# Writing out the first two and the last two steps of a software-pipelined graph network kernel

## The chip, the cores and the metric

The kernel runs on one core of one Trainium2 chip. The metric is the device time of one execution in microseconds (us), as the median of several executions. TensorE does the matrix products, VectorE the elementwise work and the transposes of 32x32 blocks, ScalarE the activations and copies with a scale, GpSimd some additions, and SyncE issues most DMAs. Each engine runs its own queue in order, and engines wait for each other by semaphores.

In the profile the engines are PE (TensorE), PEld (its weight loads), DVE (VectorE), ACT (ScalarE), POOL (GpSimd) and SP (SyncE); a trailing q, as in SPq, marks an engine's sequencer issuing DMAs. A label such as `L342` is a line of that kernel's own source. So the same statement has different line numbers in different kernels.

## The reference, cut to what matters

For each of 128 graphs with 128 nodes and 512 features (`x`), and a weighted 128x128 adjacency matrix (`adj`):

```python
h = relu(layernorm(x))
# layer 0: two hypergraph convolutions, hidden width 1024
#   conv(z, W, b) = Dinv * H @ (Binv * H.T @ (z @ W.T)) + b,   H = (adj != 0)
h = relu(conv(h, W1, b1))
h = layernorm(h, gamma, beta)
x = x + (conv(h, W2, b2) + x_in)         # x_in: what layer 0 was given
# layer 1: mean over neighbours
h = relu(layernorm(x))
out = x + relu(concat([h, adj @ h / deg]) @ W.T)
```

All is float32. The weights W1, W2 and W of layer 1 are `w1`, `w2`, `w3` below, 2 MB each.

## The kernel before

Two graphs make a pair, and there are 64 pairs (`NP`). Each weight product of a pair is done by seven block products instead of eight: `seven()` runs them in the order p1, p2, p6, p5, p7, p4, p3, with three PSUM banks A, B, C. It adds sums of weight blocks (t1 to t4), made once by `weight_sums`. Four of the products (p1, p6, p7, p4) go into A one after the other, and what stands there must be copied out before the next may write:

```python
    for name, dst, lhs, rhs, first in (
        ("p1", A, "a11", "b11", True),  ("p2", Bb, "a12", "b21", True),
        ("p6", A, "s2", "t2", False),   ("p5", Cc, "s1", "t1", True),
        ("p7", A, "s3", "t3", False),   ("fill", None, None, None, None),
        ("p4", A, "a22", "t4", False),  ("p3", Cc, "s4", "b22", False),
    ):          # ... after each: background work of other pairs, then the hook that evicts the bank
```

The smaller products between them appear in the tables by the names of their PSUM tiles: `ps_s` makes the matrix `s` of a pair from its adjacency, `pz` multiplies it with the normalised features, `py` multiplies it with the result of conv2, and `pc` multiplies beta with w2 (the beta products, once). conv1(1) is conv1 of pair 1, and so on.

So the third product (p6) waits for ScalarE's copy of p1, and ScalarE comes to that copy only when it is through with all that stands ahead in its queue.

A step `t` has three such stages: the weights of conv1 of pair t, those of conv2 of pair t-1 and those of layer 1 of pair t-2. Into each, work of other pairs is threaded as "background". Between conv1 and conv2 of a pair, the result is normalised, transposed in blocks, written to DRAM and read back as `nt`. The transpose buffer `bt` has one copy, so the second transpose of a pair waits until the first one's write has landed:

```python
    def inner_transpose(p, g):
        t = pool.tile([P, Q, B, KH], FP, tag="bt", name="bt", bufs=1)
        nc.vector.transpose(...)                          # 32x32 blocks
        d = dram.tile([P, DH], FP, tag="nd", name="n_scratch")
        nc.sync.dma_start(out=d, in_=t...)                # 512 KB
        nt = pool.tile([P, P, KH], FP, tag="nt", name="nt")
        for jj in range(Q):
            nc.sync.dma_start(out=nt[...], in_=d...)      # 4 x 128 KB
```

The schedule was a loop with a short preamble:

```python
    with tc.manual_schedule():
        load_w1(); load_w2()           # both issued by ScalarE
        load(0); load(1); load_small() # issued by SyncE: adj, adj in blocks (adjb), x
        # ... preparation of pairs 0 and 1 ...
        step(0)
        step(1, [prepare_w2, lambda: weight_sums(w3, nc.gpsimd)])
        for t in range(2, NP + 3):
            step(t)
```

Of the kernel before, what the change touches and what calls it, by code (L numbers as in the profile page):

```python
# [7 lines left out]
FP = mybir.dt.float32  # L8
# [12 lines left out]
def gnn_kernel(  # L21
# [23 lines left out]
    nc = tc.nc  # L45
# [34 lines left out]
    def load(p):  # L80
        pair = slice(2 * p, 2 * p + 2)
        ADJ[p] = pool.tile([P, 2, P], FP, tag="adj", name="adj_t")
        ADJB[p] = pool.tile([P, 2, P], FP, tag="adjb", name="adjb")
        X[p] = pool.tile([P, 2, D], FP, tag="x", name="x_t", bufs=4)
        nc.sync.dma_start(out=ADJ[p], in_=adj[pair].rearrange("g c e -> c g e"))
        load_blocks(ADJB[p], adj[pair])
        nc.sync.dma_start(out=X[p], in_=x[pair].rearrange("g c d -> c g d"))

# [12 lines left out]
    w1, w2, w3 = operands("w1", 2, 512), operands("w2", 4, 256), operands("w3", 2, 512)  # L101
    BLOCKS = (("b11", 0, 0), ("t3", 0, 1), ("b22", 1, 1), ("b21", 1, 0))

    def load_w1():
        for m, rows, cols in BLOCKS:
# [3 lines left out]
                .rearrange("(k p) h -> p k h", p=P))  # L109

    def load_small():
        nc.sync.dma_start(out=b1_bc, in_=b1.partition_broadcast(P))
        for jj in range(Q):
            for i, v in enumerate((gamma, beta)):
                src = v.rearrange("(l a) (j h) -> j a h l", a=B, j=Q)[jj]
                for h in range(2):
                    nc.sync.dma_start(out=gb[B * jj : B * (jj + 1), i, 4 * h : 4 * h + 4],
                                      in_=src[:, h, :])
        nc.sync.dma_start(out=b2_bc, in_=b2.partition_broadcast(P))

    def load_w2():
        for jj in range(Q):
            src = w2t.rearrange("(j k a) o -> j a k o", j=Q, a=B)[jj]
            for m, rows, cols in BLOCKS:
                nc.scalar.dma_start(
                    out=w2[m][B * jj : B * (jj + 1)],
                    in_=src[:, 4 * rows : 4 * rows + 4, 256 * cols : 256 * cols + 256])
# [17 lines left out]

    def prepare_w2():
        pc = small_bank("pc")
        for k in range(KH):
            betas = pool.tile([P, P], FP, tag="betas", name="betas")
            nc.vector.tensor_copy(betas, gb[:, 1, k : k + 1].to_broadcast([P, P]))  # L150
            for cols, ms in enumerate((("b11", "b21"), ("t3", "b22"))):
# [3 lines left out]
        nc.vector.tensor_copy(c0, pc)  # L155
        for m, rows in (("t3", 0), ("b11", 0), ("b22", 1), ("b21", 1)):
            for k in range(4):
                nc.scalar.activation(w2[m][:, k, :], w2[m][:, k, :], AF.Copy,
                                     scale=gb[:, 0, 4 * rows + k : 4 * rows + k + 1])
        weight_sums(w2, nc.vector)  # L160

# [95 lines left out]
    def prep_norm(p, g):  # L257
        rs = RS[1, p]
        if g == 0:
            H0[p] = pool.tile([P, 2, D], FP, tag="h0", name="h0", bufs=1)  # L260
        nc.scalar.activation(H0[p][:, g, :], X[p][:, g, :], AF.Relu,
                             bias=rs[:, 1, g : g + 1], scale=rs[:, 0, g : g + 1])
# [56 lines left out]
    def conv1_weights(p, bg, fill):  # L319
        dn = DN[p]  # L320
        ra, rb = (pool.tile([P, DH], FP, tag="r", name="r") for _ in range(2))
        R[p] = [ra, rb]
# [114 lines left out]
    def layer1_transpose(p, g):  # L437
# [6 lines left out]
        if p not in H3T:  # L444
            H3T[p] = pool.tile([P, 2, P, KD], FP, tag="h3t", name="h3t")
        for jj in range(Q):
# [69 lines left out]

    def step(t, mid=()):
        run(conv1_weights, t, [
# [9 lines left out]
        ], at(t - 3, aggregate) + at(t + 1, node_matrix))  # L528
        for f in mid:
            f()  # L530
        run(conv2_weights, t - 1, [
            at(t, inner_relu, 1) + at(t + 2, prep_adj),
            at(t, stats, 2, 1),
# [5 lines left out]
            at(t, inner_norm, 0) + at(t, inner_transpose, 1),  # L539
        ], at(t + 1, conv1_nodes))  # L540
        run(layer1_weights, t - 2, [
            at(t + 2, prep_incidence, 1) + at(t + 1, residual, 1),
# [8 lines left out]

    with tc.manual_schedule():
        load_w1()
        load_w2()
        load(0)
        load(1)
        load_small()
        prep_incidence(0, 0)
        prep_incidence(0, 1)
        stats(0, 1, 0)  # L560
        stats(0, 1, 1)
        scales(0, 1)
        prep_norm(0, 0)
        prep_norm(0, 1)
        node_matrix(0)
        weight_sums(w1, nc.vector)
        conv1_nodes(0)
        conv1_left(0)
        load_w3()
        residual(0, 1)  # L570
        residual(0, 0)
        prep_incidence(1, 0)
        prep_incidence(1, 1)
        stats(1, 1, 0)
        stats(1, 1, 1)
        scales(1, 1)
        prep_adj(0)
        prep_ant(0)
        prep_adj(1)
        step(0)  # L580
        step(1, [prepare_w2, lambda: weight_sums(w3, nc.gpsimd)])
        for t in range(2, NP + 3):
            step(t)

# [33 lines left out]
```

## Time and profile before

| | before |
|---|---|
| median time (range, runs) | 2809.39 us (2808.28 to 2809.93, 4) |
| span of the profiled execution | 2805.3 us, mean TensorE clock 0.989 |
| TensorE busy | 2706.3 us (96%) |
| first matmul / first product of conv2 of pair 1 | 11.85 / 158.90 us (159.06 in the view of the chain, which the prediction uses) |
| last pair's conv2 starts / its last stage starts | 2737.66 / 2783.01 us |

The page's overview shows where the idle time of TensorE lies. Each digit is the busy share (PE) or the granted clock (PEclk), in tenths, of one fortieth of the span, here some 70 us:

```profile
PE   3689999999999999999999999999999999999996
PEclk8899999999999999999999999999999999999998
```

Only the first three slices and the last one are not full. The prediction cuts these open.

### The profile page before, as it was taken

The numbers are of one execution on the slowest core, as the hardware profiler recorded it, in microseconds if no ns is written. First come the engines' busy times: TensorE is split into PE (matmuls) and PEld (weight loads), VectorE is DVE, ScalarE is ACT, GpSimd is POOL, SyncE is SP. The second block draws the span as 40 slices with busy tenths as digits, with TensorE's granted clock in tenths as the row PEclk, the third lists the DMA queues.
The fourth block names the chain that finished last, engine by engine and source line by source line (L and its number), as shares of the span: only waits on it lengthen the run. The fifth ranks groups of instructions, "written<-read, shape, count | busy, mean of one in ns | idle before, by whom it ended". The sixth has DMA issues, their size and how long they took to land.

```text
span 2805.3 us, 29702 instructions
## 1 busy us (share of the span) xinstructions
PE 2706.3 (96%) x8992; PEld 1702.1 (61%) x8992; DVE 2100.7 (75%) x3920; ACT 1124.3 (40%) x1745; POOL 1024.4 (37%) x922
## 2 busy tenths in 40 slices
PE   3689999999999999999999999999999999999996
PEld 1456665665665665665665665666666666666563
DVE  3677777877777777777777777777777777777753
ACT  1343443443343443343444444444444444444331
POOL 3433433433333333333333343343343343343331
PEclk8899999999999999999999999999999999999998
DMA  6233333333333333334333334333333333333321
GB/s 146 68 105 114 114 111 117 114 107 120 116 102 122 116 101 123 117 104 126 113 102 124 113 103 124 111 106 123 111 115 114 113 113 113 114 113 111 105 98 53
DMA packets 400127, 311.10 MB, mean 111 GB/s; under 512 B 166752, under 2 KB 332640, under 8 KB 399968
## 3 DMA queue, kind: packets, MB, share of 16 engines
q1 hardware_dynamic: 395808, 302.92, 35.1%
q10 hardware_dynamic: 3392, 4.20, 0.6%
q0 software_dynamic: 768, 2.10, 0.3%
q8 instruction: 72, 1.18, 0.2%
q14 instruction: 87, 0.71, 0.1%
HBM read 166.47 MB, written 142.61 MB: 110 GB/s over the span
## 4 chain that ended last, share of the span: by engine, by line
PE 94%; DMA 2%; DVE 2%; SPq 1%; issue 0%; ACT 0%; DVEq 0%; ACTq 0%
PE pA L187 46%; PE pC L187 23%; PE pB L187 11%; PE pz L301 4%; PE py L421 4%; PE pB L491 2%; PE pA L490 2%; PE ps_s L278 1%; DMA n_scratch<-bt 1%; DMA adjb<-in_adj_dram 0%; DVE bt L358 0%; DMA nt<-n_scratch 0%; DMA h_scratch<-hbt 0%; DVE st L167 0%; PE pc L152 0%
## 5 line engine op out<-in xcount | busy, mean ns | idle before, releaser
L390 POOL TENSOR_TENSOR ns<-na,ns 128x512 f32<-128x512 f32 x64 | 81.9, 1279 | 767.2 <-DVE ns L386 706.3
L187 PE MATMUL pA<-w1t,zs 128*128 128x512 f32 x512 | 246.5, 604 | 25.6 <-ACT r L339 25.5
L358 DVE STREAM_TRANSPOSE bt<-r 128x1024 f32<-128x1024 f32 x128 | 261.0, 2039 | 5.6 <-DMA n_scratch<-bt 5.6
L187 PE MATMUL pA<-w2t,ns 128*128 128x256 f32 x1024 | 242.1, 379 | 0.7 <-ACT g L409 0.7
L187 PE MATMUL pA<-w3t,hs 128*128 128x512 f32 x512 | 240.6, 592 | 0.0
L335 POOL TENSOR_TENSOR r<-r,b_bc 128x512 f32<-128x512 f32 x128 | 163.6, 1278 | 166.2 <-DVE r L333 163.5
L187 PEld LDWEIGHTS pA<-w2t,ns 128*128 128x128 f32 x1024 | 194.4, 190 | 27.8 <-ACT g L409 1.5
L348 ACT ACTIVATE r<-r 128x1024 f32<-128x1024 f32 x128 | 135.3, 1057 | 170.2 <-DVE r L343 135.3
L187 PEld LDWEIGHTS pA<-w1t,zs 128*128 128x128 f32 x512 | 98.2, 193 | 151.9 <-issue 125.7
L378 ACT ACTIVATE na<-nt 128x512 f32<-128x512 f32 x64 | 72.6, 1135 | 285.9 <-DMA nt<-n_scratch 285.9
L266 POOL TENSOR_TENSOR x_t<-x_t,b_bc 128x512 f32<-128x512 f32 x128 | 166.7, 1303 | 10.0
L187 PEld LDWEIGHTS pA<-w3t,hs 128*128 128x128 f32 x512 | 97.3, 190 | 114.9 <-issue 107.1
L167 DVE BATCH_NORM_STATS2 st<-r 128x6 f32<-128x512 f32 x256 | 162.9, 675 | 0.2 <-ACT r L348 0.2
L265 POOL TENSOR_TENSOR x_t<-x_t,h 128x512 f32<-128x512 f32 x128 | 162.8, 1272 | 0.0
L301 PE MATMUL pz<-s,h 128*128 128x128 f32 x1024 | 129.9, 281 | 32.9 <-ACT s L282 20.2
L330 POOL TENSOR_TENSOR r<-r,b_bc 128x512 f32<-128x512 f32 x64 | 81.3, 1270 | 213.0 <-DVE r L329 198.7
L352 ACT ACTIVATE r<-r,rs 128x1024 f32<-128x1024 f32 x128 | 158.2, 1236 | 0.3 <-DVE rs L175 0.3
L457 POOL TENSOR_TENSOR hs<-hs,h3t 128x256 f32<-128x256 f32 x64 | 74.2, 1160 | 225.4 <-DVE hs L455 189.1
L301 PEld LDWEIGHTS pz<-s,h 128*128 128x128 f32 x1024 | 128.4, 197 | 38.2 <-ACT s L282 20.5
L440 DVE STREAM_TRANSPOSE hbt<-h 128x512 f32<-128x512 f32 x128 | 141.5, 1118 | 7.1 <-ACT h L434 2.3
L172 ACT ACTIVATE sd<-mv,eps 128x2 f32<-128x2 f32 x192 | 56.1, 292 | 203.2 <-DVE mv L168 203.2
L187 PE MATMUL pA<-w3b,h3t 128*128 128x512 f32 x256 | 122.9, 603 | 12.9 <-DMA h3t<-h_scratch 12.9
(128 smaller groups left out, 5941.8 us busy)
## 6 DMA issues: line engine op xcount, KB each, us to landing
n_scratch<-bt SPq DMA_DIRECT2D x128, 512.0 KB, 2.7
nt<-n_scratch SPq DMA_DIRECT2D x512, 128.0 KB, 2.8
x_t<-in_x_dram SPq DMA_DIRECT2D x64, 512.0 KB, 3.7
h_scratch<-hbt SPq DMA_DIRECT2D x128, 256.0 KB, 2.1
h3t<-h_scratch SPq DMA_DIRECT2D x512, 64.0 KB, 1.9
out_dram<-x SPq DMA_DIRECT2D x64, 512.0 KB, 2.9
adj_t<-in_adj_dram SPq DMA_DIRECT2D x64, 128.0 KB, 3.1
adjb<-in_adj_dram SPq DMA_DIRECT2D x256, 32.0 KB, 2.4
```

The costliest lines, as they stand in the source:

```text
L167: nc.vector.bn_stats(st[:, i, :], src[:, i * 512 : (i + 1) * 512])
L187: nc.tensor.matmul(dst, left[lhs](k), w[rhs][:, k, :], start=(first and k == 0), stop=(k == kk - 1), skip_group_check=True)
L265: nc.gpsimd.tensor_tensor(X[p][:, g, :], X[p][:, g, :], H0[p][:, g, :], ADD)
L266: nc.gpsimd.tensor_tensor(X[p][:, g, :], X[p][:, g, :], b2_bc, ADD)
L301: nc.tensor.matmul(z[:, k * P : (k + 1) * P], h[:, g, k * P : (k + 1) * P], S[p][:, g, :], start=True, stop=True)
L335: nc.gpsimd.tensor_tensor(ra[:, h], ra[:, h], b1_bc[:, h], ADD)
L348: nc.scalar.activation(R[p][g], R[p][g], AF.Relu)
L352: nc.scalar.activation(R[p][g], R[p][g], AF.Identity, bias=rs[:, 1, g : g + 1], scale=rs[:, 0, g : g + 1])
L358: nc.vector.transpose(t.rearrange("p j b k -> p j k b"), R[p][g].rearrange("p (j k b) -> p j k b", j=Q, k=KH))
L390: nc.gpsimd.tensor_tensor(l[m], l["a12"], l["s2"], SUB)
L421: nc.tensor.matmul(py, s[:, i, :], g[:, i, :], start=True, stop=True)
L440: nc.vector.transpose(t.rearrange("p j b k -> p j k b"), H3[p][:, g, :].rearrange("p (j k b) -> p j k b", j=Q, k=KD))
```

## The change

The intent: the loop body suits the middle, but the pipe fills and drains in it badly. The changed kernel writes the first two steps (`head`) and the last two (`tail`) out by hand and keeps the loop for the rest. Five things move: ScalarE no longer issues the loads of w2; x is loaded ahead of adj; conv1 of pair 1 comes directly behind conv1 of pair 0; the scaling of w2 by gamma is threaded through conv1 of pair 1; and at the end the work between the last pair's conv2 and its last stage runs beside the products of the pair before it. Two buffers are traded: `r` gets three, `h3t` one. Two moves more are in the diff: the beta products go from behind conv1(1) to ahead of it, and the loads of w3 now stand behind `second(1, 2)`.

```diff
     def load(p):
-        nc.sync.dma_start(out=ADJ[p], in_=adj[pair]...)
-        load_blocks(ADJB[p], adj[pair])
-        nc.sync.dma_start(out=X[p], in_=x[pair]...)
+        nc.sync.dma_start(out=X[p], in_=x[pair]...)
+        load_blocks(ADJB[p], adj[pair])
+        nc.sync.dma_start(out=ADJ[p], in_=adj[pair]...)
 ...
     def load_small():        # 8 small loads of gamma and beta instead of 16, b2 last
 ...
     def load_w2():
-                nc.scalar.dma_start(
+                nc.sync.dma_start(
 ...
-        ra, rb = (pool.tile([P, DH], FP, tag="r", name="r") for _ in range(2))
+        ra, rb = (pool.tile([P, DH], FP, tag="r", name="r", bufs=3) for _ in range(2))
 ...
-            H3T[p] = pool.tile([P, 2, P, KD], FP, tag="h3t", name="h3t")
+            H3T[p] = pool.tile([P, 2, P, KD], FP, tag="h3t", name="h3t", bufs=1)
 ...
+    def head():
+        load_w1(); load(0); <b1>; load(1); load_w2(); load_small()
+        <statistics, incidence and norm of pair 0>
+        node_matrix(0); conv1_nodes(0); weight_sums(w1, nc.vector); conv1_left(0)
+        conv1_weights(0, <background: residual of pair 0, preparation of pair 1>)
+        conv1_nodes(1); conv1_left(1)
+        <two relus, statistics, scale of pair 0>
+        beta_products()
+        <norms and transposes of pair 0>
+        conv1_weights(1, <background: the four scalings of w2, preparation of pair 2, w2 sums>)
+        conv2_left(0, ...)
+        second(1, 2)
+        load_w3(); weight_sums(w3, nc.gpsimd); prep_ant(2); prep_adj(3)
+        third(1)
+    def tail(t):
+        conv2_nodes(t - 1)
+        run(layer1_weights, t - 2, <background: conv2_out, statistics, norm, transposes of pair t-1>)
+        aggregate(t - 2); layer1_left(t - 1); finish(t - 2)
+        layer1_weights(t - 1, ...); aggregate(t - 1); finish(t - 1)
 ...
-        step(0)
-        step(1, [prepare_w2, lambda: weight_sums(w3, nc.gpsimd)])
-        for t in range(2, NP + 3):
-            step(t)
+        head()
+        for t in range(2, NP):
+            first(t); second(t); third(t)
+        first(NP); second(NP); tail(NP)
```

More of the change, by code (lines that the diff above doesn't have):

```diff
@@ L81, in load @@
         pair = slice(2 * p, 2 * p + 2)
+        X[p] = pool.tile([P, 2, D], FP, tag="x", name="x_t", bufs=4)
+        ADJB[p] = pool.tile([P, 2, P], FP, tag="adjb", name="adjb")
         ADJ[p] = pool.tile([P, 2, P], FP, tag="adj", name="adj_t")
-        ADJB[p] = pool.tile([P, 2, P], FP, tag="adjb", name="adjb")
-        X[p] = pool.tile([P, 2, D], FP, tag="x", name="x_t", bufs=4)
+        nc.sync.dma_start(out=X[p], in_=x[pair].rearrange("g c d -> c g d"))
+        load_blocks(ADJB[p], adj[pair])
         nc.sync.dma_start(out=ADJ[p], in_=adj[pair].rearrange("g c e -> c g e"))
-        load_blocks(ADJB[p], adj[pair])
-        nc.sync.dma_start(out=X[p], in_=x[pair].rearrange("g c d -> c g d"))
     b1_bc = const.tile([P, DH], FP, name="b1_bc")
@@ L101, in gnn_kernel @@
     w1, w2, w3 = operands("w1", 2, 512), operands("w2", 4, 256), operands("w3", 2, 512)
-    BLOCKS = (("b11", 0, 0), ("t3", 0, 1), ("b22", 1, 1), ("b21", 1, 0))
+    BLOCKS = (("b11", 0, 0), ("b21", 1, 0), ("t3", 0, 1), ("b22", 1, 1))
     def load_w1():
@@ L111, in load_small, with vector_of @@
     def load_small():
-        nc.sync.dma_start(out=b1_bc, in_=b1.partition_broadcast(P))
         for jj in range(Q):
-            for i, v in enumerate((gamma, beta)):
-                src = v.rearrange("(l a) (j h) -> j a h l", a=B, j=Q)[jj]
-                for h in range(2):
-                    nc.sync.dma_start(out=gb[B * jj : B * (jj + 1), i, 4 * h : 4 * h + 4],
-                                      in_=src[:, h, :])
+            for i, v in enumerate((beta, gamma)):
+                nc.sync.dma_start(
+                    out=gb[B * jj : B * (jj + 1), i].rearrange("a (l h) -> a l h", h=2),
+                    in_=v.rearrange("(l a) (j h) -> j a l h", a=B, j=Q)[jj])
         nc.sync.dma_start(out=b2_bc, in_=b2.partition_broadcast(P))
+    def vector_of(i, k):
+        c = 2 * (k % 4) + k // 4
+        return gb[:, i, c : c + 1]
     def load_w2():
@@ L124, in load_w2 @@
             for m, rows, cols in BLOCKS:
-                nc.scalar.dma_start(
+                nc.sync.dma_start(
                     out=w2[m][B * jj : B * (jj + 1)],
@@ L144, in gnn_kernel, with beta_products @@
     c0 = const.tile([P, D], FP, name="c0")
-    def prepare_w2():
-        pc = small_bank("pc")
+    def beta_products():
+        pc = bank("pc")
         for k in range(KH):
             betas = pool.tile([P, P], FP, tag="betas", name="betas")
-            nc.vector.tensor_copy(betas, gb[:, 1, k : k + 1].to_broadcast([P, P]))
+            nc.vector.tensor_copy(betas, vector_of(0, k).to_broadcast([P, P]))
             for cols, ms in enumerate((("b11", "b21"), ("t3", "b22"))):
@@ L155, in prepare_w2, with scale_w2 @@
         nc.vector.tensor_copy(c0, pc)
-        for m, rows in (("t3", 0), ("b11", 0), ("b22", 1), ("b21", 1)):
-            for k in range(4):
-                nc.scalar.activation(w2[m][:, k, :], w2[m][:, k, :], AF.Copy,
-                                     scale=gb[:, 0, 4 * rows + k : 4 * rows + k + 1])
-        weight_sums(w2, nc.vector)
+    def scale_w2(m, rows):
+        for k in range(4):
+            nc.scalar.activation(w2[m][:, k, :], w2[m][:, k, :], AF.Copy,
+                                 scale=vector_of(1, 4 * rows + k))
     def ln_stats(src, mv, tag):
@@ L258, in prep_norm @@
         rs = RS[1, p]
-        if g == 0:
+        if p not in H0:
             H0[p] = pool.tile([P, 2, D], FP, tag="h0", name="h0", bufs=1)
@@ L515, in run, with first @@
                 f()
-    def step(t, mid=()):
+    def first(t):
         run(conv1_weights, t, [
@@ L528, in step, with second @@
         ], at(t - 3, aggregate) + at(t + 1, node_matrix))
-        for f in mid:
-            f()
+    def second(t, adj_of=None):
         run(conv2_weights, t - 1, [
-            at(t, inner_relu, 1) + at(t + 2, prep_adj),
+            at(t, inner_relu, 1) + at(t + 2 if adj_of is None else adj_of, prep_adj),
             at(t, stats, 2, 1),
@@ L540, in step, with third @@
         ], at(t + 1, conv1_nodes))
+    def third(t):
         run(layer1_weights, t - 2, [
@@ L550, in step @@
         ], at(t - 1, conv2_nodes))
-    with tc.manual_schedule():
+    def head():
         load_w1()
+        load(0)
+        nc.sync.dma_start(out=b1_bc, in_=b1.partition_broadcast(P))
+        load(1)
         load_w2()
-        load(0)
-        load(1)
         load_small()
+        for g in range(2):
+            stats(0, 1, g)
+        scales(0, 1)
         prep_incidence(0, 0)
         prep_incidence(0, 1)
-        stats(0, 1, 0)
-        stats(0, 1, 1)
-        scales(0, 1)
-        prep_norm(0, 0)
-        prep_norm(0, 1)
+        for g in range(2):
+            prep_norm(0, g)
@@ L565, in gnn_kernel @@
         node_matrix(0)
+        conv1_nodes(0)
         weight_sums(w1, nc.vector)
-        conv1_nodes(0)
         conv1_left(0)
-        load_w3()
-        residual(0, 1)
-        residual(0, 0)
-        prep_incidence(1, 0)
-        prep_incidence(1, 1)
-        stats(1, 1, 0)
-        stats(1, 1, 1)
-        scales(1, 1)
-        prep_adj(0)
-        prep_ant(0)
-        prep_adj(1)
-        step(0)
-        step(1, [prepare_w2, lambda: weight_sums(w3, nc.gpsimd)])
-        for t in range(2, NP + 3):
-            step(t)
+        conv1_weights(0, [
+            at(0, residual, 1) + at(0, residual, 0) + at(1, prep_incidence, 0),
+            at(1, prep_incidence, 1),
+            at(1, stats, 1, 0),
+            at(1, stats, 1, 1) + at(1, scales, 1),
+            at(0, prep_adj) + at(2, load),
+            at(1, prep_norm, 1),
+            at(1, prep_norm, 0),
+            [],
+        ], at(1, node_matrix))
@@ new lines, in head @@
+        conv1_nodes(1)
+        conv1_left(1)
+        inner_relu(0, 1)
+        stats(0, 2, 1)
+        inner_relu(0, 0)
+        stats(0, 2, 0)
+        scales(0, 2)
+        beta_products()
+        for g in (1, 0):
+            inner_norm(0, g)
+            inner_transpose(0, g)
+        conv1_weights(1, [
+            [lambda: scale_w2("b11", 0)] + at(0, prep_ant),
+            at(2, prep_incidence, 0) + at(2, prep_incidence, 1) + at(1, prep_adj) + at(3, load),
+            [lambda: scale_w2("t3", 0)] + at(2, stats, 1, 0),
+            at(2, stats, 1, 1) + at(2, scales, 1),
+            [lambda: scale_w2("b22", 1)] + at(1, residual, 1) + at(1, residual, 0),
+            [lambda: scale_w2("b21", 1)],
+            [lambda: weight_sums(w2, nc.vector)],
+            at(1, prep_ant),
+        ], at(2, node_matrix))
@@ new lines, in head @@
+        conv2_left(0, "a11", "a12", "s1", "s3", "s2", "s4", "a22")
+        second(1, 2)
+        load_w3()
+        weight_sums(w3, nc.gpsimd)
+        prep_ant(2)
+        prep_adj(3)
+        third(1)
+    def tail(t):
+        p = t - 1
+        conv2_nodes(p)
+        run(layer1_weights, t - 2, [
+            [],
+            at(p, conv2_out, 1) + at(p, conv2_out, 0) + at(p, stats, 3, 1) + at(p, stats, 3, 0),
+            at(p, scales, 3),
+            at(p, layer1_norm, 1) + at(p, layer1_norm, 0),
+            at(p, layer1_transpose, 1) + at(p, layer1_transpose, 0),
+            [],
+            [],
+            [],
+        ], [])
+        aggregate(t - 2)
+        layer1_left(p)
+        finish(t - 2)
+        layer1_weights(p, [[]] * 8, [])
+        aggregate(p)
+        finish(p)
@@ L587 @@
+    with tc.manual_schedule():
+        head()
+        for t in range(2, NP):
+            first(t)
+            second(t)
+            third(t)
+        first(NP)
+        second(NP)
+        tail(NP)
 _OUT = ((128, 128, 512), "float32")
```

## The prediction

> **What bounds the kernel now.** I first cut the span into three stretches, in the view of busy time by stretch (per engine: busy us and instructions; then TensorE clock, DMA share, GB/s).
>
> ```profile
> 0.00:160.00 160.00, 84.01 (x246) 50.52 (x247) 82.18 (x159) 42.70 (x72) 60.23 (x57) 0.85 0.42 109
> 160.00:2710.00 2550.00, 2549.86 (x8536) 1608.12 (x8535) 1982.01 (x3700) 1063.71 (x1645) 951.66 (x854) 1.00 0.36 113
> 2710.00:2806.00 96.00, 72.39 (x213) 43.48 (x212) 36.52 (x63) 17.89 (x28) 12.54 (x12) 0.92 0.20 68
> ```
>
> The middle is solid TensorE work at full clock (2549.86 of 2550 us). It can't get faster by reordering. What there is to win is 160 - 84.0 = 76.0 us of idle TensorE in the head, 96 - 72.4 = 23.6 in the tail (5.3 of them after its last matmul, 0.7 past the end), and the half-clock loss. For the last, the head's products at full clock, by durations from the middle of the chain: 3 x 0.45 (ps_s), 3 x 1.78 (pz), 21 x 1.72 (conv1), 7.16 (pc), 7 x 1.73 (conv2), 1.72 (py) = 63.8, against 84.0 spent. So 20 us go to the clock.
>
> Then what TensorE waited for in the head (total, times, longest) and in the tail:
>
> ```profile
> PE pA L187 <- ACT r L339: 25.5, 3, 13.2
> PE pz L301 <- ACT s L282: 20.2, 1, 20.2
> PE pz L301 <- ACT h L261: 12.7, 3, 6.1
> PE ps_s L278 <- DVE sb L255: 11.8, 1, 11.8
> ```
> ```profile
> PE pA L187 <- DMA h3t<-h_scratch: 12.9, 1, 12.9
> ```
>
> The 20.2 comes from ScalarE, which issues the w2 loads before its first activation (timeline):
>
> ```profile
> 29.41 1.28 ACT L172 ACT_TABLE_LOAD   x1 [29.41 <-DMA b_bc<-in_b_dram]
> 31.43 1.52 ACT L261 ACTIVATE h<-x_t,rs 128x512 f32<-128x512 f32 x2 [0.43 <-DVE rs L175]
> ```
>
> The other waits are order: the copy L339 stands in ScalarE's queue behind a square root or a copy of `nt` that is itself waiting. The chain of waits shows the `nt` detour, from the second transpose to the copy:
>
> ```profile
> 77.24 2.05 DVE bt L358
> 79.31 3.36 DMA n_scratch<-bt
> 83.99 2.95 DMA nt<-n_scratch
> 87.99 0.68 ACT r L339
> ```
>
> **What the Trainium skill says.** "TensorE: Matmul & The Clock Gate", Part 1: the clock falls to half after about one idle window of 3.4 us and comes back after about as long a busy one. The trace agrees: after the 12.9 us wait the first four matmuls of the last pair took 3.66 us, against 1.72 for four in the chain. "DMA: Bandwidth & Descriptors", Anatomy of one DMA: a fixed cost of about 2 us, mostly the receipt; the trace has 2.0 to 2.2 for `h_scratch`, 2.6 to 3.4 for `n_scratch`. Same page, Issuing engines are not separate DMA queues: moving a load to another queue only saves issue time. The trace agrees with the second half: the gain is ScalarE's freedom, not bandwidth (mean DMA share 0.98 from 10 to 20 us). Same page, Queues, rings and completion order: each DMA engine alternates between rings packet by packet; the 128-byte packets of `adjb` next to the 2 KB packets of w1 fit that: issued from 1.2 us, the last landed only at 9.2.
>
> **The change, part by part.** I list when stages begin, by durations of before; (n) is the pair.
>
> Start: x goes first, and ScalarE is free after w1 (about 5.5 us). x lands near 6, so statistics (1.7), square root and norm are done by 10.5, before the incidence. `adjb` now queues behind x on its ring, beside w1: I take 10.0 (estimate: 2.6 MB at the 344 GB/s seen from 4 to 8 us). Plus 2.3 on VectorE (9.50 to 11.80 before): ps_s(0) at 12.3, and 1.2 + 0.5 later pz(0) at 14.0. Before 33.3: 19.3 saved.
>
> conv1(0): zs2 ended 7.4 after pz began, so the third product starts at 22 instead of 45.6, as no square root of pair 1 is ahead of the copy now. Five products, ps_s and a copy: ends 31.8.
>
> pz(1) needs h0(1). h0 has one buffer, read by pair 0's residual on GpSimd, whose second instruction needs b2. b2 is now the last small load, behind 2 MB of w2 on one queue whose issues wait for the landing of the eighth before. I put it at 31 (29.4 before: w2 is paced at 206 GB/s from about 17 us, then eight small loads). Then 2 x 1.27 + 1.5 (two norms): pz(1) at 35.1, before 66.5.
>
> pz(1) at half clock 4.1; za copies, two relus (2 x 1.06), statistics (2 x 1.4), scale: betas at 45.1. TensorE cools again, so pc takes 7.2 + 2: conv1(1) starts at 54.4. The transposes now stand behind c0: 55.3, then 2.05 + 2.7 + 2.05 and 7.65 from the end of the second to `nt` (79.29 to 86.94 before): 69.7.
>
> conv1(1): five products, 62.9. ps_s(2) and the square root of pair 2 stand behind the second transpose (62.05) on VectorE: 0.45 + 2.3 + 1.5 + 0.75 + 1.7, then on ScalarE 0.3, four scalings of w2 (4 x 0.51) and the copy 0.7: the next product waits till 71.7, runs cold (3.65), and the stage ends at 77.1. conv2(0) starts then; before 109.0.
>
> conv2(0): ns2 stands behind the w2 sums (one beside GpSimd takes 3.2, not 1.2): third product at 83.5, last ends 93.9, py waits for GpSimd's sum: conv1(2) starts at 97.5, before 135.3.
>
> conv1(2) keeps the `nt` detour: second transpose about 98.4 to 100.4, but adj(3)'s scratch write and four reads now sit ahead on the sync queue (3.4 more): `nt` at 110.9, third product 112.6, before 146.95. From there as before (12.1): conv2(1) at 124.7 instead of 159.06. **Head: 34.4 us.** From there the order is the old one, and TensorE stays full.
>
> Tail: py goes before layer1 of the last but one pair (waits 1.2 net for GpSimd), and conv2_out, statistics, norm and transposes of the last pair run beside its products. First transpose ends near 2765.0 instead of 2773.3. The load of `h3t` now waits for its single buffer, read until the sixth product (2768.5): then 1.75 + 2.2 + 0.1 + 1.7 + 2.0: the last pair's first product at 2776.2 instead of 2783.0. From there 22.3 us, as before. **Tail: 6.8 us**, with some chance of another 1.9 if the 4.3 us gap leaves the clock up; I take 7.
>
> Sum: 34.4 + 7 = 41.4; 2808.9 - 41.4 = 2767.5, said 2767.
>
> **Rivals.** (a) b2 lands by 27: pz(1) starts at 31.8, with no cold start; 5 to 6 us more, 2762. For: 29.4 before with twice as many small loads. Against: it was not behind w2 in one queue. (b) b2 lands at 36 to 40: every stage after it moves along, 2772 to 2776. For: eight-deep gating, each w2 load 5.5 us to landing. (c) The single `h3t` buffer stalls the middle: 61 steps at even 1 us would make it slower, 2828. Against: the load was issued at 2704.3 while the last reader was done by about 2694; 10 us of slack. (d) The chained queue waits in conv1(1) and conv2(0) do not bind, or bind less: TensorE has 60 us of work there, so with 30 us of idle the middle would begin at 95 and the time be near 2740, over 2% faster. Against: each engine runs its queue in order, and the second transpose can't start before the first one's DMA has landed. (e) w3's sixteen issues (8.6) and sums (10.6) sit on GpSimd ahead of pair 2's bias sums: I get 125.4 for the first, just in time; if late by 5, 2772.
>
> **Range and chances.** The middle is measured, to a few us. The head is a chain of some fifteen links, each good to about 1 us, with b2 good to 4 and the clock windows to 2 per cold start; the tail is good to 2. I take 2754 to 2780. Over 2% faster needs 56 us (below 2752.7), possible only with (a) and much of (d): 0.07. Slower by 2% needs (c) at its worst: 0.01.
>
> **What would show it.** Right: first matmul at 12 us, pz(0) near 14, the last long wait of the head over near 113 and TensorE full from there, h3t wait of the last pair near 4 us, the middle still full. pz(1) waiting for ScalarE h, and that for GpSimd's residual, at about 35. Wrong: a TensorE idle share inside the middle, ps_s(0) later than 14, or no wait at pc.

## The result, and the profile after

| | before | after |
|---|---|---|
| median (range, runs) | 2809.39 us (2808.28 to 2809.93, 4) | 2776.55 us (2774.55 to 2778.63, 4) |
| span of the profiled execution | 2805.3 us | 2772.7 us |
| mean TensorE clock | 0.989 | 0.992 |

The outputs are right. The ratio is 0.9884, with a 95% interval of 0.9867 to 0.9901: 1.2% faster, which counts as the same at the 2% mark. Ratios here are the mean time of one kernel's fast runs over the mean of the other's fast runs of the same rounds, so they are not quite the ratio of the medians quoted. The medians of the kernel before varied from 2807.7 to 2809.8 between the calls.

The gain can be split at one event which both traces have, the first product of the last pair's conv2: it starts at 2737.66 before and at 2711.91 after, so 25.75 us came from the head and the middle. From there to the end it is 67.62 before and 60.79 after, so 6.83 us came from the tail. Together these are the 32.6 us between the spans. The view of busy time by stretch says that none of it came from the middle (columns: stretch, its length, then busy us and instructions of PE, PEld, DVE, ACT and POOL, the clock, the DMA share and GB/s):

```profile
0.00:130.00 130.00, 74.77 (x232) 46.67 (x232) 76.81 (x151) 40.60 (x69) 58.94 (x54) 0.84 0.52 128
130.00:2680.00 2550.00, 2549.77 (x8537) 1608.54 (x8538) 1982.82 (x3703) 1067.20 (x1648) 950.62 (x855) 1.00 0.36 113
2680.00:2773.00 93.00, 77.33 (x225) 45.59 (x223) 40.39 (x68) 19.09 (x30) 15.52 (x14) 0.97 0.22 76
```

The middle is as full as before (2549.77 of 2550 us); its first stage, conv2(1), begins 25.1 us earlier (133.77 for 158.90). But 55 us are still idle in the first 130. The waits of TensorE in the first 165 us, and then the one that counts in the tail (total, times, longest), answer to the two lists in the prediction:

```profile
PE pA L190 <- ACT r L342: 18.5, 1, 18.5
PE ps_s L281 <- DVE sb L258: 15.1, 2, 13.6
PE pc L155 <- DVE betas L153: 6.6, 1, 6.6
PE pA L190 <- ACT r L331: 5.9, 3, 5.2
PE pz L304 <- ACT h L264: 4.3, 1, 4.3
PE pA L190 <- DVE ns L389: 3.1, 1, 3.1
```
```profile
PE pA L190 <- DMA h3t<-h_scratch: 4.3, 1, 4.3
```

The wait of 20.2 us for ScalarE's copy of `s` is gone. The reason is in ScalarE's timeline, where the table load now stands at 7.37 us instead of 29.41, right behind the four loads of w1:

```profile
7.37 1.28 ACT L175 ACT_TABLE_LOAD   x1 [7.37 <-DMA w1b<-in_w1t_dram]
9.39 1.52 ACT L264 ACTIVATE h<-x_t,rs 128x512 f32<-128x512 f32 x2 [0.43 <-DVE rs L178]
```

But one wait is larger than expected: 18.5 us for the copy L342, ahead of the third product of conv1 of pair 2, where the times of the prediction leave 11.7. The chain of waits (start, length, what) shows what that copy waited for:

```profile
97.81 2.62 DMA n_scratch<-bt
102.33 5.85 DMA an_scratch<-adj_t
...
110.08 4.91 DMA n_scratch<-bt
116.31 4.35 DMA nt<-n_scratch
120.76 1.14 ACT na L381
121.91 0.58 ACT r L342
122.53 3.42 PE pA L190 x4
```

Read it from below: the product waits for a copy, the copy stands behind another copy of `nt`, that waits for the load of `nt`, that for the second scratch write, and that stood on the queue behind the reads of pair 3's adjacency. The write `n_scratch`, which took 2.62 us at 97.81, took 4.91 at 110.08. In between lies something new: GpSimd issued the sixteen loads of w3 from 99.31 to 109.3 us. From 103 to 109 us the mean DMA share was 1.08, against 0.52 over the first 130 us. The change itself put them there: in the kernel before they began with this line and were all issued by 49.9 us.

```profile
41.37 0.68 POOL L133 DMA_DIRECT2D w3b<-in_wt_dram  x1
```

This is where the stages stand, by the starts of TensorE's products:

| stage starts at (us) | before | predicted | after | off by |
|---|---|---|---|---|
| ps_s of pair 0 | 11.85 | 12.3 | 13.55 | +1.2 |
| pz of pair 0 | 33.27 | 14.0 | 15.25 | +1.2 |
| pz of pair 1 | 66.47 | 35.1 | 36.82 | +1.7 |
| pc (beta products) | | 45.1 | 47.04 | +1.9 |
| conv1(1), p1 | | 54.4 | 55.68 | +1.3 |
| conv1(1), p4 | | 71.7 | 71.82 | +0.1 |
| conv2(0), p6 | | 83.5 | 85.00 | +1.5 |
| conv1(2), p1 | 135.28 | 97.5 | 100.39 | +2.9 |
| conv1(2), p6 | 146.95 | 112.6 | 122.53 | +9.9 |
| conv2(1), p1 | 158.90 | 124.7 | 133.77 | +9.1 |

The first eight rows are off by 3 us at most. Seven of the missing microseconds appear between two rows, in the detour of `nt` through DRAM.

### The profile page after: what moved, and what is told of

Read it like the earlier page. It is cut to its first block, busy times and chain, and to the rows that moved or that the text cites. A ratio compares the mean times of both kernels' runs of the same rounds, so it can differ in the third digit from the quotient of the medians.

```text
span 2772.7 us, 29639 instructions
## 1 busy us (share of the span) xinstructions
PE 2701.9 (97%) x8992; PEld 1700.8 (61%) x8992; DVE 2100.0 (76%) x3920; ACT 1126.9 (41%) x1745; POOL 1025.1 (37%) x922
## 4 chain that ended last, share of the span: by engine, by line
PE 95%; DMA 2%; DVE 1%; issue 0%; SPq 0%; ACT 0%; POOL 0%; ACTq 0%; DVEq 0%; POOLq 0%
PE pA L190 47%; PE pC L190 23%; PE pB L190 12%; PE pz L304 4%; PE py L424 4%; PE pB L494 2%; PE pA L493 2%; PE ps_s L281 1%; DMA n_scratch<-bt 0%; DMA w2b<-in_w2t_dram 0%; DMA w1t<-in_w1t_dram 0%; PE pc L155 0%; DMA an_scratch<-adj_t 0%; DMA h_scratch<-hbt 0%; DMA adjb<-in_adj_dram 0%
## 5 line engine op out<-in xcount | busy, mean ns | idle before, releaser
L190 PE MATMUL pA<-w1t,zs 128*128 128x512 f32 x512 | 242.5, 596 | 18.5 <-ACT r L342 18.5
L190 PEld LDWEIGHTS pA<-w2t,ns 128*128 128x128 f32 x1024 | 195.4, 191 | 31.4 <-ACT r L351 3.5
L484 ACT ACTIVATE oa<-pA 128x512 f32<-128x512 f32 x64 | 38.2, 597 | 235.0 <-PE pA L190 235.0
```

The costliest lines, as they stand in the source:

```text
L190: nc.tensor.matmul(dst, left[lhs](k), w[rhs][:, k, :], start=(first and k == 0), stop=(k == kk - 1), skip_group_check=True)
```

## The experiments

Theory A was: the w3 transfers crowd the `nt` detour of pair 1, and the small loads, b2 above all, are late by their place in the queue. The rival B was: the detour has these latencies anyway, or the scratch of pair 3 ahead of it on the queue is what costs. Twelve kernels ran, each timed with five rounds beside the kernel before on the same chip. All were correct. In the tables "p6" is the start of the third product of conv1(2).

### e1: Load w3 earlier

```diff
         conv1_left(1)
+        load_w3()
 ...
         second(1, 2)
-        load_w3()
         weight_sums(w3, nc.gpsimd)
```

> The sixteen loads of w3 are issued by GpSimd right after the left operands of pair 1 (about 43 us) instead of at 99 us; nothing else moves. Theory A (the 2 MB of w3 share the DMA engines with pair 1's way through DRAM, and make it slow): adj(3)'s scratch write lands in about 2.2 us instead of 5.85, the second n_scratch in 2.8 instead of 4.9, the last nt in 3.0 instead of 4.35; the third product of conv1(2) starts near 115 instead of 122.5, and the time falls by about 7 us, to 2769.5. Rival B (these transfers are slow, or queued, for the order on the sync queue alone): durations and the wait of 18.5 us stay within 1 us, time 2776.

Measured: 2774.06 us (2772.74 to 2775.25), ratio 0.9875. The transfers did as theory A says: from the end of the second transpose to the first copy of `nt` it took 7.0 us (110.59 to 117.55) instead of 17.6 (103.19 to 120.76); adj(3)'s own transfers were nearly through by then. This puts w3's loads back to where the kernel before had them (42.4 to 51 us). Yet p6 came only 3.2 us earlier, at 119.30, and the time fell by 2.5. The second transpose began 7.4 us later than in the changed kernel: 1.9 because conv1(2) itself began later (102.28), after two products at a low clock in conv2(0), and the rest by a new cost ahead of the transpose. Compare VectorE's timeline in the changed kernel,

```profile
99.63 0.43 DVE L235 TENSOR_TENSOR adj_t<-adj_t,deg 128x256 f32<-128x256 f32 x1
99.98 0.41 DVE L254 TENSOR_REDUCE cnt<-adjt 128x2 f32<-128x256 f32 x1
100.42 0.17 DVE L256 TENSOR_SCALAR cnt<-cnt 128x2 f32<-128x2 f32 x1
100.83 0.43 DVE L258 TENSOR_TENSOR sb<-adjt,cnt 128x256 f32<-128x256 f32 x1
```

with that of this experiment (start, length, then the instruction), where w3 had landed and GpSimd made its four sums from 101.22 to 110.85:

```profile
101.53 2.32 DVE L235 TENSOR_TENSOR adj_t<-adj_t,deg 128x256 f32<-128x256 f32 x1
103.78 0.41 DVE L254 TENSOR_REDUCE cnt<-adjt 128x2 f32<-128x256 f32 x1
104.22 1.86 DVE L256 TENSOR_SCALAR cnt<-cnt 128x2 f32<-128x2 f32 x1
106.31 2.32 DVE L258 TENSOR_TENSOR sb<-adjt,cnt 128x256 f32<-128x256 f32 x1
```

Three of the four were held up, by 1.7 to 1.9 us each and 5.5 in all, beside GpSimd sums of 2.33 to 2.42 us; one of these three works on two numbers per partition. Only the reduction was untouched. The Trainium skill, page "SBUF — State Buffer", section Who interferes with whom, fits: VectorE and GpSimd share a pair of ports as an exclusive lock, an operation with two SBUF inputs or in a two-port mode waits for the other engine's whole instruction, `tensor_scalar` can be one of these, and on trn2 `tensor_reduce` never contends. The trace agrees, with 0.43 to 2.32, 0.17 to 1.86 and 0.41 to 0.41 us. In the changed kernel the same sums ran from 113.1 to 122.6, when VectorE was waiting anyway.

### e2: Pair 3's adjacency later

```diff
-        prep_adj(3)
         third(1)
+        prep_adj(3)
```

> The row-normalised adj of pair 3 is written to and read from DRAM after pair 1's second transpose instead of before it; the w3 loads stay at 99 us. Rival B (order on the sync queue is the whole cost): the second n_scratch is issued near 103.3 instead of 110.1 and with plain latencies of 2.7 and 3.0 the third product of conv1(2) starts near 113, 9 us earlier, time 2767. Theory A: the issue is as early, but n_scratch and nt still take 4.9 and 4.3 us beside w3, so it starts near 116, 6.5 us earlier, time 2770.

Measured: 2774.74 us (2772.95 to 2775.22), ratio 0.9876. p6 started at 119.41. Both forecasts were too early, theory A's (116, 2770) less so than B's (113, 2767). Nothing stood ahead of the second scratch write any more, and it was issued right after its transpose, at 103.6; but it landed only at 110.3, 6.7 us later, while w3 was in flight:

```profile
103.61 0.34 SPq L364 DMA_DIRECT2D n_scratch<-bt  x1
110.34 1.73 SPq L367 DMA_DIRECT2D nt<-n_scratch  x4
117.66 1.13 ACT L381 ACTIVATE na<-nt 128x512 f32<-128x512 f32 x1 [12.25 <-DMA nt<-n_scratch]
```

So it is not the place on the queue alone. From the end of the transpose (103.6) to the copy of `nt` (117.7) it took 14.1 us, 3.5 less than in the changed kernel, as the prediction had it for adj(3). But that leaves it 7 longer than without w3. Rival B falls as the main cause.

### e3: b2 first among the small loads

```diff
         nc.sync.dma_start(out=b1_bc, in_=b1.partition_broadcast(P))
+        nc.sync.dma_start(out=b2_bc, in_=b2.partition_broadcast(P))
         load(1)
 ...       # and no longer at the end of load_small()
```

> The load of b2 goes right behind that of b1, ahead of pair 1's loads and of w2. If the wait for b2 on GpSimd (8.0 us, which holds h0 of pair 1) sets the stages after it: b2 lands before 20 us, pz(1) starts near 32.4 instead of 36.8 with the clock still up, pc near 41.5 instead of 47.0, conv1(2) near 95, and the time falls by about 5 us, to 2771.5. Rival: a later wait swallows it (w2, or the detour of pair 1 through DRAM at 100 to 120 us): pz(1) is as early but conv1(2)'s third product stays near 122 and the time at 2776.

Measured: 2770.88 us (2769.31 to 2772.63), ratio 0.9864, 5.7 us less than the changed kernel. In the changed kernel GpSimd's timeline had this line (in brackets, the idle time before it and what ended it):

```profile
32.73 1.26 POOL L269 TENSOR_TENSOR x_t<-x_t,b_bc 128x512 f32<-128x512 f32 x1 [8.04 <-DMA b_bc<-in_b_dram]
```

Now the wait is gone and pz of pair 1 starts at 32.97, directly behind conv1(0) and at full clock: its sixteen matmuls took 1.95 us instead of 3.62. By the trace p6 moved from 122.53 to 118.64, so 3.9 us arrive in the middle; the 5.7 of the medians are good to about 2. (The spans of the two traces differ by 1.9 only, as this profile was the slowest run of its four and that of the changed kernel the fastest.)

### e4: The last pair's h3t in another buffer

```diff
-            H3T[p] = pool.tile([P, 2, P, KD], FP, tag="h3t", name="h3t", bufs=1)
+            if p == NP - 1:    # nt is free by then and has two buffers
+                H3T[p] = pool.tile([P, 2, P, KD], FP, tag="nt", name="h3t")
+            else:
+                H3T[p] = pool.tile([P, 2, P, KD], FP, tag="h3t", name="h3t", bufs=1)
```

> Only the last pair's h3t lies in a free buffer of nt, so that its load need not wait for the sixth product of the pair before. If that wait costs: the first load is issued near 2741.1 instead of 2742.8 (in the times of the changed kernel's trace), the last pair's first product starts 1.6 us earlier (wait 2.7 instead of 4.3 us), perhaps with less half-clock time; time 1.6 to 3.5 us less. Rival: the second half of h3t, not the first, decides, and it is paced by the sync queue alone: no change.

Measured: 2775.56 us (2771.51 to 2778.42), ratio 0.988. In time this is within the scatter, so the expected 1.6 to 3.5 is neither shown nor refuted by it. The trace shows the wait of the last pair for `h3t` at 2.3 us instead of 4.3, and 32.9 us instead of 34.6 from the last p7 of the pair before to the end. So the single buffer costs just under 2 us in the changed kernel. A version with two `h3t` buffers beside three `r` buffers doesn't fit: the build needed 119.2 kB per partition for that pool where 115.8 were left. So the second `h3t` buffer paid for the third `r`.

### e5: w3 earlier, its sums later

As the first experiment, but the sums after conv1(2):

```diff
-        weight_sums(w3, nc.gpsimd)
         prep_ant(2)
 ...
             first(t)
+            if t == 2:
+                weight_sums(w3, nc.gpsimd)
             second(t)
```

> As e1 (w3's loads right after conv1_left(1)), but w3's sums on GpSimd go from before prep_ant(2) to after conv1(2). Theory: in e1 half of the gain was lost because the sums ran on GpSimd beside VectorE's work of pair 1 and slowed it (statistics and incidence 2.3 us instead of 0.4), so the second transpose came at 108.6 instead of 101.2. With the sums away it should start near 103, nt land near 112 and the third product of conv1(2) start near 114 instead of 119.3 in e1 and 122.5 in the changed kernel: 5 us less than e1, about 2769. Rival: the VectorE times in e1 come from the w3 transfers and not from the sums; then the second transpose stays near 108 and the time at 2774.

Measured: 2776.31 us (2775.77 to 2777.68), ratio 0.989: no gain over the changed kernel, and worse than with the sums early. This was a miss in the time and a hit in part of the mechanism. The second transpose started at 104.68 instead of 108.55 (said 103) and p6 at 117.43 instead of 119.30 (said 114). The way from the transpose to the copy of `nt` took 9.0 us instead of 7.0, as the second scratch write now stood behind adj(3)'s transfers until 108.15. But the sums, now beside conv2(1), slowed VectorE there and made a new wait of 3.1 us at pz of pair 3, and the product after it ran cold. What was won was given back 20 us later.

### e6: The three head edits together, sums after conv1(2)

```diff
 # e1, e2 and e3 together, and w3's sums as in e5
+        nc.sync.dma_start(out=b2_bc, ...)   # right after b1
+        load_w3()                            # right after conv1_left(1)
+        prep_adj(3)                          # right after third(1)
+        if t == 2: weight_sums(w3, nc.gpsimd)   # in the loop, after first(t)
```

> The three head edits together (w3 loads early, adj(3)'s degree work after the third stage, b2's load right after b1's) with w3's sums after conv1(2). Theory: the nt detour of pair 1 then has no competing transfers and no slowed VectorE, and everything is 5 us earlier by b2: second transpose near 97, nt near 105, third product of conv1(2) near 107 instead of 122.5; 15 us less than the changed kernel, 2761 to 2764. Rival: the waits only move on (w3's sums or adj(3) late hold up conv2(1) or the third stage of pair 0): 2767 to 2770.

Measured: 2767.47 us (2766.03 to 2768.95), ratio 0.9858. p6 starts at 108.85, 13.7 us earlier than in the changed kernel and near the expected 107. The second transpose ended at 99.7, and the `nt` detour is short again, 7.4 us to the copy:

```profile
99.71 3.14 DMA n_scratch<-bt
104.17 2.91 DMA nt<-n_scratch
107.10 1.12 ACT na L380
```

But the time fell by 9.1 only. The difference is the rival's: the wait that appeared in the run before is here too.

```profile
133.77 1.89 PE L303 MATMUL pz<-s,h 128*128 128x128 f32 x8 [3.14 <-ACT h L263]
135.45 2.87 PE L189 MATMUL pA<-w2t,na 128*128 128x256 f32 x8
```

The bracket gives the idle 3.14 us, for a norm that stands behind VectorE's statistics; the next eight products took 2.87 us instead of 1.89. That is 3.1 + 1.0 of the missing 4.6.

### e7: The old tail

```diff
-        first(NP)
-        second(NP)
-        tail(NP)
+        for t in range(NP, NP + 3):
+            first(t)
+            second(t)
+            third(t)
```

> Changed head, but the last two steps by the loop as before (the single h3t buffer and the third r buffer stay). Theory: the tail's 6.8 us are an own, additive part, so the time is 2783 and the wait of the last pair for h3t is again near 13 us. Rival: with the single h3t buffer the old order waits longer still, since its load can't start before the last reader is through: 2785 or more; or the tail's gain was not from the order: 2777.

Measured: 2784.04 us (2782.45 to 2785.26), ratio 0.9917, 7.5 us more than the changed kernel. From the first product of the last pair's conv2 to the end it is 67.66 us, as before (67.62), and the old wait is back, although `h3t` still has a single buffer:

```profile
2760.70 3.77 PE L190 MATMUL pA<-w3b,h3t 128*128 128x512 f32 x4 [12.87 <-DMA h3t<-h_scratch]
```

So the tail's gain comes from the order alone and adds to the head's.

### e8: w2 issued by ScalarE again

```diff
     def load_w2():
-                nc.sync.dma_start(
+                nc.scalar.dma_start(
```

> Changed kernel, but the sixteen w2 loads are issued by ScalarE again, after w1's. Theory: the copy of S and the norm of pair 0 stand behind these issues until about 29, so pz(0) starts near 33 instead of 15.3; pz(1) then follows conv1(0) with no wait for b2 (which is early on the sync queue), near 51 instead of 36.8; the rest moves along: 12 to 14 us slower, 2789 to 2791. Rival: pz(1) is bound by the landing of w2 and b2 anyway and the later stages by their own chains, so most of it is hidden: under 6 us, 2778 to 2782.

Measured: 2791.25 us (2789.63 to 2793.07), ratio 0.9942, 14.7 us more than the changed kernel. ScalarE's first activation is late again:

```profile
28.89 1.28 ACT L175 ACT_TABLE_LOAD   x1 [28.89 <-DMA w2b<-in_w2t_dram]
```

pz of pair 0 starts at 34.96 instead of 15.25, 19.7 us later; pz of pair 1 at 52.79 instead of 36.82, 16.0 later, as b2 is no longer what it waits for. This one word in the diff is the largest single part of the gain that was measured by itself.

### e9: w3's sums on VectorE, inside the detour

The three head edits and the separate last `h3t`, with the sums right behind the second transpose of pair 1:

```diff
-        third(1)
+        third(1, [lambda: weight_sums(w3, nc.vector)])   # run after inner_transpose(1, 0)
         prep_adj(3)
```

> As e6 (b2 early, w3 loads early, adj(3) late), but w3's sums are made by VectorE right behind the second transpose of pair 1, inside the nt detour, where VectorE has little to do; and the last pair's h3t in an nt buffer as in e4. Theory: e6's new wait of TensorE at pz of pair 3 (3.1 us, with a cold start after it) came from the sums on GpSimd slowing VectorE's statistics; it is gone here, so 4 us less than e6, and about 1 for the tail: 2761 to 2763. Rival: the sums now delay VectorE's own statistics and ns2 of pair 1, and the third product of conv1(2) or conv2(1) waits 3 to 5 us for them instead: 2766 to 2768.

Measured: 2760.84 us (2760.2 to 2763.36), ratio 0.9835, which is 15.7 us less than the changed kernel by the medians and 0.5% by the two ratios. TensorE's waits from 95 to 150 us are now these:

```profile
PE pA L189 <- ACT r L341: 9.4, 1, 9.4
PE py L423 <- POOL g L407: 1.5, 1, 1.5
PE pA L189 <- ACT r L330: 0.4, 1, 0.4
```

There is no wait at pz any more, and TensorE is full from 109 us on. p6 starts at 108.86, as in the run of e6, though the second transpose ended 1.4 us earlier; so the sums, 7.0 us of VectorE's time, cost 1.4 us where they now lie, and the 4 us at pz are saved. In the chain of this trace it is they that end last: sums, statistics and a square root (106.93) stand directly ahead of the copy of `nt` (107.13). Neither VectorE nor GpSimd is free of the other here: VectorE's three sums took 1.62, 2.17 and 3.25 us and GpSimd's one 3.32 instead of 2.34.

### e10: The beta products earlier

As the run before, and:

```diff
         conv1_left(1)
+        beta_products()
 ...
         scales(0, 2)
-        beta_products()
```

> e9 with the beta products right after conv1_left(1), before the two relus, statistics and scale of pair 0. Theory: TensorE then runs pc straight after pz(1) without the 6.6 us wait and without a cold start, near 37 to 44, while ScalarE copies; conv1(1) starts near 45 instead of 50, and the first transposes, no longer behind the copy of c0 at the end of pc, come about 3 to 5 earlier too: 3 to 5 us less than e9, 2757 to 2760. Rival: the order of the two transposes and their trips through DRAM set the end of conv1(1), and pair 0's statistics now wait for the eight beta copies, so it gives nothing: within 1 us of e9.

Measured: 2761.47 us (2760.01 to 2761.76), ratio 0.9834: nothing, as the rival said. The first half of the theory held. pc ran from 36.89 and mostly at full clock, the wait for the betas fell from 7.2 to 1.9, and conv1(1) started at 43.90 instead of 50.93. But the third product got a wait in its place:

```profile
53.45 3.52 PE L189 MATMUL pA<-w1t,zs 128*128 128x512 f32 x4 [5.95 <-ACT r L341]
```

Without the edit this product started at 54.36. ScalarE's copy stands behind two norms and four scalings of w2, the norms behind the statistics, and those now behind the eight beta copies. Of 7 us, 0.9 was left here and 0.7 at p6.

### e11: Two r buffers

```diff
-        ra, rb = (pool.tile([P, DH], FP, tag="r", name="r", bufs=3) for _ in range(2))
+        ra, rb = (pool.tile([P, DH], FP, tag="r", name="r", bufs=2) for _ in range(2))
```

> Changed kernel with two r buffers instead of three. Theory: the first copy of conv1(1) then waits for the second transpose of pair 0 (about 64), so the third product starts near 65 instead of 59; but the sixth waits until 71.8 for ScalarE's copy behind the square root of pair 2 anyway, so the loss is 0 to 2 us: 2776.5 to 2778.5, and the middle stays full, as it was before with two. Rival: the third buffer is what lets the first three stages overlap: 5 us or more, 2781 and up.

Measured: 2776.43 us (2775.84 to 2776.64), ratio 0.9888. The third buffer is worth nothing. The working was partly wrong: the copy waits for the first transpose, not the second, so it starts at 58.36 instead of 57.60 and p6 of conv1(1) waits 0.2 us, not 6. The conclusion stands, and since this buffer took the place of the second `h3t`, the trade in the change bought nothing and cost the tail just under 2 us, by the trace of e4 (two `r` with two `h3t` in the changed order were not run).

### e12: The old order of each pair's loads

```diff
-        <x>; load_blocks(ADJB[p], adj[pair]); <adj>
+        <adj>; load_blocks(ADJB[p], adj[pair]); <x>
```

> Changed kernel with each pair's loads in the order of before (adj, adjb, x) and everything else as changed. Theory: adjb lands about 2 earlier (9 instead of 11.2), but x about 3 later (9.5 to 10 instead of 6.4), and VectorE has the statistics, which need x, ahead of the incidence; so ps_s(0) starts at 14 to 15.5 instead of 13.55 and pz(0) 1 to 2 later, and most of that is lost again in pz(1)'s wait for b2, which doesn't depend on it: 0 to 1 us slower, 2776 to 2778. Rival: the order is worth what ps_s(0) shows, and b2 moves too: 2 us or more, 2779 and up.

Measured: 2776.28 us (2774.98 to 2778.68), ratio 0.988: no difference, as expected. The start was later than I gave it: the statistics waited for x until 12.59, so ps_s began at 17.38 instead of 13.55, and the products of conv1(0) up to the sixth came 3.8 us later. But pz of pair 1 started at 38.61 instead of 36.82, without a gap and warm, and pc at 47.16 instead of 47.04. The wait for b2 had swallowed nearly all of it: 4.3 us of idle time and a cold start on one side, 3.8 us of a later start on the other.

## Why the prediction was right or wrong

The class, the range and the mechanism held, but for one term of the head; the centre, 2767, was 9.5 us too low. Of the signs that it lists, one clearly failed, "the last long wait of the head over near 113": it was over at 122.5. The first matmul (13.55, said 12) and pz(0) (15.25, said 14) were over 1 us late.

**The middle.** "It can't get faster by reordering": right, 2549.77 of 2550 us.

**The sums.** The list of the head's products at full clock, 63.8 us, leaves out one of four ps_s and the first 1.1 us of conv2(1), so some 18.5 us went to the clock, not 20; nothing later rests on it.

**The start.** Taking w2 off ScalarE brought what the prediction's first step says (pz of pair 0 at 15.25, 18.0 us earlier than before; said 19.3). The run that undoes it alone costs 14.7 us at the end, so about that much of the head's 25.75 hangs on it. The estimate for the landing of `adjb`, 10.0, was 1.2 us short of the 11.2 measured; it mattered little, as a shift of 3.8 us at this point was absorbed.

**b2.** Put at 31, landed at 32.7, so rival (b), 36 to 40, did not come true. The 29.4 given for the kernel before is a misreading: it is the start of ScalarE's table load, which the profile puts down to b2. b2 was issued at 26.19 there and took 5.2 us to land, which makes it 31.4. The step that pz of pair 1 waits for it through GpSimd's residual was right, and rival (a), 5 to 6 us for an early b2, was made true by one moved line: 5.7 us by the medians, 3.9 by the trace.

**The chained queues.** Rival (d), that they do not bind, failed as the prediction argued. Every product from pz of pair 1 to conv2(0) is within 2 us of the list. Moving the beta products 7 us up gave nothing, because the queue behind them did not move.

**The step that failed** is "conv1(2) keeps the `nt` detour: second transpose about 98.4 to 100.4, but adj(3)'s scratch write and four reads now sit ahead on the sync queue (3.4 more): `nt` at 110.9". The mechanism is there, but its term, 10.5 us from the end of the transpose to `nt`, measured 17.6. The prediction took durations of before for the transfers and counted w3 only as work of GpSimd, in rival (e). What w3 did was to fill the DMA engines: 2 MB in flight beside a chain of dependent small transfers. The runs give the term piece by piece: 7.4 us with neither w3 nor adj(3) in the way (e6; said 7.65), 14.1 with w3 alone (e2), 17.6 with both. So adj(3) costs 3.5 (said 3.4), and w3's crowding the 6.7 that the sum lacked. The fourth case, adj(3) without w3, is e5: 9.0 us, where adj(3) had a longer start on the transpose. With the start that it had in the changed kernel, e5's durations (4.6 us from adj(3)'s issue to the scratch write's, 7.5 from there to the copy) give 11.2, an estimate near the 10.5 said. The split depends on when the transfers meet, so it is good to about 1 us. w3's 6.7 are most of the 8.65 us by which the head fell short; the other 2 us lie ahead of conv1(2), in small misses such as b2's and a cold start in conv2(0).

**Rival (e)** had the right object and the wrong way: the sums on GpSimd did not hold up TensorE in the changed kernel. They do so as soon as w3 lands earlier, through VectorE.

**The tail.** 6.8 us said, 6.83 measured by the spans, 7.5 by the undo. The h3t wait was given as near 4 and is 4.3. The hope that a 4.3 us gap leaves the clock up failed: the first product behind it took 3.50 us.

**Rival (c)**, the single h3t buffer stalling the middle, did not come true.

What stays open: after the w2 queue, some 11 us of the head's gain belong to the new order of the stages and to the threaded scaling of w2. These were not undone one by one, so this share is a difference and not a measurement. The best version still waits 9.4 us at p6. Of these 1.4 belong to the sums on VectorE, the rest to the `nt` detour; no run here shortened it further.

**Better than both:** the version with b2 early, w3 loaded early and summed on VectorE inside the detour, adj(3) late and the last h3t apart runs at 2760.84 us, 1.65% under the kernel before.

## What to carry to other kernels

When a pipe fills, one-time loads should be placed by what is in flight beside them, not only by when they are needed: a bulk load beside a chain of small dependent transfers stretched every link of it here (the writes from 2.6 to 4.9 us and from 2.7 to 5.9, the read from 2.9 to 4.4). A side job such as a weight sum belongs into a stretch where the engine it disturbs is waiting anyway; moving it elsewhere can give back all that was won. Before valuing a speed-up at one point, look for the next fixed arrival downstream (here b2): up to it, early and late starts end at the same time.

## What the Trainium skill lacked or had wrong

- "DMA: Bandwidth & Descriptors", Anatomy of one DMA, gives the time of one DMA alone (on the path that GpSimd issues), and Queues, rings and completion order tells how rings alternate; neither says what a chain of dependent transfers pays beside a bulk load of another queue. Here a 512 KB scratch write took 2.6 us alone and 4.9 to 6.7 us beside the 2 MB of w3, and the way from a transpose through DRAM to the first use 14.1 instead of 7.4.
- "SBUF — State Buffer", Who interferes with whom, has the rule right; it gives no time for a tiny operation. Here a `tensor_scalar` on two numbers per partition went from 0.17 to 1.86 us beside GpSimd's sums.
- "TensorE: Matmul & The Clock Gate", Part 1, names an idle window of about 3.4 us. A gap of 2.3 us ahead of the last pair was followed by two slow products (2.88 and 2.82 us, granted clock 0.72 and 0.63) in e4 and by none (2.08 and 1.88) in e9; in e10 a gap of 2.4 us was followed by one of 3.76. The page says that the window runs free, but a gap shorter than it isn't safe either. (Its own second failure mode speaks of frequent micro-idles, without a length.)
